# Filling TensorE's longest planned pauses with products that nobody reads, in a kernel whose order is written by a planner

## The chip, the core and the metric

The kernel runs on one core of one Trainium2 chip. The metric is the device time of one execution in microseconds (us). The median of six runs before the change is 1732.15 us, and the six lie between 1729.69 and 1736.9 us. One further execution was recorded by the hardware profiler, and every row below is from it.

The names of the engines are those of the profile: PE is TensorE's matmul unit and PEld its weight load, DVE is VectorE, ACT is ScalarE, POOL is GpSimd, SP is SyncE, which issues most DMAs. POOL issues the indirect DMAs (gathers by a list of row numbers).

## The reference

Four layers run over 64 sequences of 64 tokens, 128 features wide (4096 tokens). Each layer adds a gated cross-attention over a context and then a gated feed-forward network (FFN):

```
x = x + tanh(g_xattn[l]) * attention_l(layernorm(x), context)
x = x + tanh(g_ffn[l])   * ffn_l(layernorm(x))            # l = 0, 1, 2, 3
```

Layers 0 and 1 attend with 16 heads, layer 2 with 8, layer 3 has a resampler that attends to context and latents together. The FFNs are mixtures of experts: layer 0 has 32 small experts with 6 of them per token, layer 1 and layer 2 have 8 with 2 per token, layer 3 has 4 with 2 per token and a layernorm inside each. All of it is float32.

## The kernel before

The 4096 tokens are cut in 8 blocks of 512 (4 tiles of 128 tokens). `attention_16`, `gated_ffn`, `attention_8`, `attention_lat` and `ffn_3` each do one layer's step for one block. `sparse_ffn`, the FFN of layer 1, works on a group of two blocks, four groups in all. It sorts the tokens by expert with small matrix products and DVE operations (`slots_of`): the last of these products, `pid`, sums 16 products of 128x128 with 128x24 and gives the list `z_rows`, by which POOL gathers the rows of each expert into `zs`. TensorE transposes `zs` (into `pt`), multiplies it with the expert's weights (`g`, `u`, `po`), the result goes to DRAM (`oD`), and later 16 gathers per group fetch the results `back`.

**The planner.** No engine is called at once. The `Plan` object records every operation, and at the end `order()` simulates the five engines with costs written in the kernel: it takes the next operation of each engine by a key, holds tiles back until a buffer is free, charges 1.5 times for TensorE in the first 3.4 us after a pause of over 1.7 us, and notes when each operation would start (`starts`). An operation is one call or one `unit` of several calls on one engine, for example the four transposes of a block; its `us` is the sum of the calls' planned costs. `issue()` then calls the engines in the order of the planned starts:

```
    def issue(self):
        with self.tc.manual_schedule():
            for i in self.order():
                for bound, args, kw in self.ops[i].calls:
                    bound(*args, **kw)
```

Each engine works through its own instructions strictly in that order. An instruction waits on semaphores for its inputs and for the release of the buffer that it writes. Since all calls to the engines are made in this one place, almost every row of the profile has line L435, and rows are told apart by the names of the tiles.

**PSUM.** TensorE writes to PSUM. `ps(name)` takes one of six banks of 128x512 float32, `ps_two` the one double bank of the attention scores. A bank goes back to the pool when its last reader is done. The names that matter below: `pc` is the transposed context of a block, `pt` holds transposes, `pvar` the variances of the last FFN, `ph` its hidden layer, `po` an output projection, `g` and `u` the two halves of a gated hidden layer, and `acc` the running output of an FFN.

**How a product looks in the profile.** A float32 product takes two rows of PE and two of PEld (two passes); a transpose takes one. `masks` is a constant tile whose first 128 columns are the identity.

Of the kernel before, what the change touches and what calls it, by code (L numbers as in the profile page):

```python
# [20 lines left out]
P = 128  # L21
# [162 lines left out]
class Plan:  # L184
# [244 lines left out]
        return "no operation can start:\n" + "\n".join(lines)  # L429

    def issue(self):
        with self.tc.manual_schedule():
            for i in self.order():
                for bound, args, kw in self.ops[i].calls:
                    bound(*args, **kw)  # L435


SWITCH = 3.0
COLD, PAUSE, SLOWER = 3.4, 1.7, 1.5


class PlanEngine:
# [14 lines left out]
def flamingo_kernel(ctx: ExitStack, tc: tile.TileContext, a: dict, out: bass.AP):  # L457
    nc = Plan(tc)
# [37 lines left out]
    def load(name, shape=None, at=0.0, t=None):  # L496
        src = a[name]
        if t is None:
            t = const.tile(list(shape or src.shape), F32, tag=name, name=name, bufs=1)
        nc.sync.dma_start(t[: src.shape[0]], src, not_before=at)  # L500
        return t
# [14 lines left out]
    def source_tile(name):  # L516
        t = const.tile([C + 1, TOK], F32, tag=name, name=name)
        nc.gpsimd.memset(t[C : C + 1, :], 1.0)
        return t
# [14 lines left out]
    with nc.stage(0.0, 1.0):  # L534
# [4 lines left out]
        masks = load("masks")  # L539
# [46 lines left out]
        load_ffn(3, at=T_LOAD + 150)  # L586

    with nc.stage(0.0, 1.0):
        ident = masks[:, 0:128]
        head8 = masks[:, 128:136]  # L590
        half2 = masks[:, 136:138]
        ones = const.tile([P, P], F32, tag="ones", name="ones")
        nc.vector.memset(ones, 1.0)
        zeros = const.tile([1, 1], mybir.dt.bfloat16, tag="zero", name="zero")
        nc.vector.memset(zeros, 0.0)
        zero = zeros.to_broadcast([1, 512])
        minus_half = const.tile([P, 16], F32, tag="minus_half", name="minus_half")
        nc.vector.memset(minus_half, -0.5)

        cn_tiles = [source_tile(f"cn{i}") for i in range(2)]  # L600
        ctx_tiles = [source_tile(f"ctx{i}") for i in range(2)]
        cn_d = dram.tile([C, B * S], F32, tag="cn_d", name="cn_d", bufs=1)
        y_d = dram.tile([P, B * S], F32, tag="y_d", name="y_d", bufs=1)
        k8_d = dram.tile([P, 4 * B * S], F32, tag="k8_d", name="k8_d", bufs=1)
        v8_d = dram.tile([P, 4 * B * S], F32, tag="v8_d", name="v8_d", bufs=1)
        gates = const.tile([P, 8], F32, tag="gates", name="gates")
        nc.scalar.activation(gates, rows[:, 0:8], AF.Tanh)
# [1280 lines left out]
```

## Time and profile before

| what | value |
|---|---|
| median of the runs | 1732.15 us |
| the profiled execution, its own time | 1730.78 us |
| its span, first to last instruction | 1729.0 us |
| PE busy | 1587.9 us, 92% of the span, 14369 rows |
| DVE, POOL, ACT busy | 61%, 54%, 50% |
| mean granted TensorE clock | 0.961 |

The profiled execution's own time is 1.78 us over its span and 1.37 us under the median, so that a difference worked out on its rows can be added to the median. PE's share of busy time is an average over stages. In the page's 40 slices of 43 us PE is at 0.9 or more nearly everywhere, and falls to 0.6 to 0.8 in the first slice, in five slices from about 735 to 950 us, and in the last two. "Granted clock" is the share of full speed that the throttle gave TensorE; in the trace it takes two values, 1 and one half.

### The profile page before, as it was taken

The page shows a single profiled execution, that of the slowest core. Times are in us where ns is not written, and L with a number is a line of the kernel's source. Part 1 is how long each engine was busy: PE and PEld are TensorE (multiplying, and loading weights), DVE is VectorE, ACT ScalarE, POOL GpSimd, SP SyncE. Part 2 cuts the span into 40 slices and gives each one's busy share as a digit, 9 for nine tenths or more (in the row PEclk, how much of TensorE's full clock was granted, in tenths as well). Part 3 has the DMA queues.
Part 4 walks back from the last instruction along what each step waited for, and adds up shares of the span by engine and source line. Part 5 has one row for each costly group of instructions (what it writes and reads, how often), then busy time and mean ns, then how long its engine had stood idle before and what let it go on. Part 6 is the DMA issues. An engine that isn't in the chain of part 4 may idle for free. (4 is left out here: it accounts for less than half of the span.)

```text
span 1729.0 us, 37328 instructions
## 1 busy us (share of the span) xinstructions
PE 1587.9 (92%) x14369; PEld 1096.0 (63%) x14369; DVE 1063.3 (61%) x2933; ACT 858.5 (50%) x1289; POOL 928.8 (54%) x906
## 2 busy tenths in 40 slices
PE   6999999999999999978769599999999999899976
PEld 3556556556566656557758487766767786677654
DVE  5864777786678565762746366684655475575652
ACT  3563776666757575622324264444443553454422
POOL 7464555565654745322373555686553666654741
PEclk9999999999999999988889799999999999999998
DMA  7231160324030321465577362521152323220211
GB/s 230 96 118 60 59 192 27 117 98 119 27 123 30 102 85 55 154 205 126 148 231 192 100 215 53 181 95 56 37 159 88 103 63 117 83 89 2 81 32 38
DMA packets 107786, 180.94 MB, mean 105 GB/s; under 512 B 22964, under 2 KB 53016, under 8 KB 103128
## 3 DMA queue, kind: packets, MB, share of 16 engines
q1 hardware_dynamic: 102488, 168.06, 30.7%
q0 software_dynamic: 5120, 10.50, 3.1%
q8 instruction: 113, 1.85, 0.5%
q14 instruction: 65, 0.53, 0.1%
HBM read 146.71 MB, written 35.26 MB: 105 GB/s over the span
## 5 line engine op out<-in xcount | busy, mean ns | idle before, releaser
L435 DVE TENSOR_TENSOR h<-h,u 128x512 f32<-128x512 f32 x224 | 150.9, 685 | 216.8 <-PE u L435 137.4
L435 POOL TENSOR_TENSOR h<-h,pb 128x512 f32<-128x512 f32 x128 | 161.3, 1273 | 199.5 <-DVE h L435 99.6
L435 ACT ACTIVATE h<-g 128x512 f32<-128x512 f32 x224 | 132.6, 597 | 229.3 <-PE g L435 202.0
L435 ACT ACT_TABLE_LOAD x159 | 204.0, 1283 | 29.6 <-issue 9.1
L435 POOL TENSOR_TENSOR ln_r<-ln_ve,minus_half 128x4 f32<-128x4 f32 x64 | 66.7, 1042 | 215.6 <-DVE ln_ve L435 214.2
L435 PEld LDWEIGHTS acc<-w_L,h 128*128 128x128 f32 x1088 | 134.9, 191 | 42.6 <-issue 29.8
L435 PEld LDWEIGHTS acc<-L_w,h 128*128 128x128 f32 x1088 | 133.6, 192 | 33.0 <-issue 24.2
L435 PE MATMUL acc<-w_L,h 128*128 128x128 f32 x1088 | 144.2, 278 | 0.9 <-POOL h L435 0.7
L435 PE MATMUL acc<-L_w,h 128*128 128x128 f32 x1088 | 142.5, 278 | 0.8 <-issue 0.4
L435 PE MATMUL g<-zTm,w_L 128*128 128x512 f32 x272 | 141.8, 604 | 0.3 <-ACT cn L435 0.3
L435 PE MATMUL u<-zTm,w_L 128*128 128x512 f32 x272 | 140.1, 599 | 0.1
L435 DVE TENSOR_REDUCE top<-sc 128x16 f32<-128x1024 f32 x80 | 97.5, 1218 | 63.7 <-PE sc L435 32.7
L435 POOL TENSOR_TENSOR kb<-kT,masks 128x1024 f32<-128x1024 f32 x64 | 120.9, 1904 | 24.3 <-ACT kT L435 8.6
L435 POOL DMA_INDIRECT zs<-zD,z_rows x96 | 92.7, 965 | 75.3 <-DVE z_rows L435 23.8
L435 POOL TENSOR_SCALAR z<-x,ln_mv,ln_r 128x128 f32<-128x128 f32 x160 | 127.9, 811 | 4.4 <-DMA zs<-cT 0.8
L435 ACT COPY prT<-pt 128x512 f32<-128x512 f32 x176 | 95.9, 593 | 46.8 <-PE pt L435 44.1
L435 POOL TENSOR_TENSOR pb<-zTm,pb 128x512 f32<-128x512 f32 x64 | 80.0, 1271 | 45.3 <-DMA pb<-cD 43.3
L435 ACT ACTIVATE pr<-pr 128x1024 f32<-128x1024 f32 x88 | 93.0, 1057 | 17.0 <-DVE pr L435 16.2
L435 PEld LDWEIGHTS pt<-masks,pr 128*128 128x128 f32 x704 | 80.1, 142 | 31.7 <-issue 21.5
L435 PE MATMUL pt<-masks,pr 128*128 128x128 f32 x704 | 97.3, 276 | 2.8 <-POOL pr L435 1.0
L435 POOL TENSOR_TENSOR pr<-pr,rs 128x512 f32<-128x512 f32 (+1 forms) x40 | 47.8, 1211 | 81.3 <-DVE rs L435 59.2
L435 POOL DMA_INDIRECT back<-oD,rows_of x64 | 63.2, 988 | 44.0 <-issue 25.0
(299 smaller groups left out, 3381.0 us busy)
## 6 DMA issues: line engine op xcount, KB each, us to landing
wt<-experts SPq DMA_DIRECT2D x96, 384.0 KB
pb<-cD SPq DMA_DIRECT2D x256, 128.0 KB
pb<-cD SPq DMA_DIRECT2D x96, 256.0 KB
k_d<-kS SPq DMA_DIRECT2D x8, 1024.0 KB
v_d<-vS SPq DMA_DIRECT2D x8, 1024.0 KB
kT<-k_d SPq DMA_DIRECT2D x8, 1024.0 KB
v<-v_d SPq DMA_DIRECT2D x8, 1024.0 KB
oD<-zs SPq DMA_DIRECT2D x32, 192.0 KB
```

Of the source, the lines that this page charges most:

```text
L435: bound(*args, **kw)
```

## The change

`issue()` keeps the planned end of the last TensorE operation (`done`). Before each TensorE operation it looks at the planned pause since then. If the pause is 3.0 us or longer, the tile that the operation writes first has two dimensions, and the operation doesn't add to an earlier sum, then `keep_busy` issues int((pause - 1.0) / 0.25) products ahead of it. Each multiplies the identity with itself (128 rows by up to 128 columns on both sides) and is written to the first columns of the bank that the operation writes next, which overwrites it. No other operation, order or cost is changed, and the planner doesn't know of the products.

```
     def issue(self):
+        done = 0.0
         with self.tc.manual_schedule():
             for i in self.order():
-                for bound, args, kw in self.ops[i].calls:
+                op = self.ops[i]
+                if op.eng == "PE":
+                    if done > 0.0:
+                        self.keep_busy(op, self.starts[i] - done)
+                    done = self.starts[i] + op.us
+                for bound, args, kw in op.calls:
                     bound(*args, **kw)
+
+    def keep_busy(self, op, pause):
+
+        dst = op.calls[0][1][0]
+        if pause < LONG or len(dst.shape) != 2 or not op.calls[0][2].get("start", True):
+            return
+        m, n = dst.shape[0], min(dst.shape[1], P)
+        for _ in range(int((pause - IDLE) / FILL)):
+            self.tc.nc.tensor.matmul(
+                dst[:, 0:n], lhsT=self.filler[:, 0:m], rhs=self.filler[:, 0:n], start=True, stop=True
+            )
 
 
 SWITCH = 3.0
 COLD, PAUSE, SLOWER = 3.4, 1.7, 1.5
+LONG, IDLE, FILL = 3.0, 1.0, 0.25
...
-        ident = masks[:, 0:128]
+        ident = nc.filler = masks[:, 0:128]
```

## The prediction

> **What bounds the kernel now.** The page first, then TensorE's waits, then its timeline around the longest of them.
>
> ```profile
> PE 1587.9 (92%) x14369; PEld 1096.0 (63%) x14369; DVE 1063.3 (61%) x2933; ACT 858.5 (50%) x1289; POOL 928.8 (54%) x906
> PEclk9999999999999999988889799999999999999998
> ```
>
> TensorE is the bound nearly everywhere. Its idle time is 1729.0 - 1587.9 = 141 us. A clock of 0.961 means (1 - 0.961) x 2 x 1729 = 135 us at half speed, so better warmth could never give more than 67 us. The waits (us in total, times, longest):
>
> ```profile
> PE g L435 <- ACT zs L435: 17.0, 5, 14.9
> PE ph L435 <- DVE zs L435: 15.4, 2, 8.1
> PE pt L435 <- DMA zs<-zD,z_rows: 10.6, 3, 6.5
> PE pid L435 <- issue: 8.5, 1, 8.5
> ```
>
> Which pauses are filled follows from the planner's starts, which the kernel before computes too. Eight planned pauses last 3 us or more; one (`pv` in `context_8`) has three dimensions and drops out. The other seven, in order, with planned pause and number of products, and in brackets TensorE's real pause there: A `pc` of block 0, 5.1 us, 16 (0.4 at 9.54 us); B `pid` of the second group, 9.7 us, 34 (8.49); C the next `pt`<-`zs`, 10.4 us, 37 (6.53); D a `pt` of `attention_8`, 4.1 us, 12 (none, at 989.96); E a `pvar`, 4.5 us, 14 (0.1, at 1598.83); F a `ph`, 7.5 us, 25 (8.10, at 1673.64); G the last such `ph`, 6.6 us, 22 (7.26, at 1704.13). That is 160 products, 320 rows. In all but A, whose bank is new, and E, the bank's last reader ends before TensorE falls idle, so the products start at once.
>
> When does the clock fall? The granted clock changes on a grid of 3.41 us; these stretches are such windows (columns: length, busy time by engine, clock):
>
> ```profile
> 905.50:908.90 3.40, 1.38 (x6) 0.55 (x5) 0.91 (x6) 3.36 (x5) 1.89 (x2) 1.00 0.65 162
> 1417.50:1420.90 3.40, 1.99 (x7) 0.79 (x5) 3.12 (x17) 0.58 (x2) 0.10 (x2) 1.00 0.69 77
> 1670.10:1673.50 3.40, 0.00 (x0) 0.00 (x0) 0.68 (x1) 0.00 (x0) 3.32 (x5) 0.50 0.76 242
> 1673.50:1677.00 3.50, 3.36 (x4) 1.40 (x5) 2.09 (x4) 0.60 (x1) 3.48 (x4) 0.51 0.18 67
> ```
>
> After the first (PE busy 1.38 of 3.40, 41%) the next window is at half, after the second (59%) it isn't. After one window that is full (the last) the clock is back. So TensorE must be busy for about half of every window.
>
> Around B and C (first DVE, which needs `pid`; then PE alone):
>
> ```profile
> 868.21 0.18 DVE L435 CAST z_rows<-pid 128x24 int32<-128x24 f32 x1 [7.18 <-remote]
> ```
>
> ```profile
> 846.94 1.16 PE L435 MATMUL acc<-shared,h 128*128 128x128 f32 x8
> 856.59 6.99 PE L435 MATMUL pid<-ids,match 128*128 128x24 f32 x32 [8.49 <-issue]
> 863.41 2.05 PE L435 MATMUL acc<-shared,h 128*128 128x128 f32 x8
> 872.00 0.48 PE L435 MATMUL pt<-masks,zs 128*128 128x128 f32 x1 [6.53 <-DMA zs<-zD,z_rows]
> 874.11 0.48 PE L435 MATMUL pt<-masks,zs 128*128 128x128 f32 x1 [1.64 <-issue]
> 877.65 0.47 PE L435 MATMUL pt<-masks,zs 128*128 128x128 f32 x1 [3.07 <-DMA zs<-zD,z_rows]
> ```
>
> `pid` ends at 863.58, yet DVE sees it only at 868.21. POOL runs 16 `back` gathers without a break from 845.41 to 866.02. The same beside another run of gathers (801.90 to 809.19), where TensorE had nothing to wait for:
>
> ```profile
> 804.95 0.65 PE L435 MATMUL av<-prT,values 128*32 128x64 f32 x32
> 805.42 0.40 PE L435 MATMUL av<-prT,sums_w 128*32 128x128 f32 x6
> 806.13 0.39 PE L435 MATMUL av<-prT,sums_w 128*32 128x128 f32 x2 [0.32 <-issue]
> 807.55 0.38 PE L435 MATMUL av<-prT,sums_w 128*32 128x128 f32 x2 [1.03 <-issue]
> 808.97 0.38 PE L435 MATMUL av<-prT,sums_w 128*32 128x128 f32 x2 [1.04 <-issue]
> 810.37 0.67 PE L435 MATMUL av<-prT,sums_w 128*32 128x128 f32 x4 [1.02 <-issue]
> ```
>
> In the middle of one unit TensorE drops to two rows per 1.42 us, and recovers 1.2 us after the last gather. I counted its rows from the first gather of a run until this starts: 53 here, 57 from 1110.09, 50 from 1432.59, 48 from 946.95, 49 from 941.08, 72 from 1178.36. So beside a run of gathers TensorE gets about 50 rows, then crawls, and its results are seen late. What holds it, the trace doesn't say.
>
> **The change part by part.** A pass of 128x128 starts every 0.1115 us at full clock and 0.213 at half (`acc` rows); one product costs 0.223 or 0.427 us. Nothing is removed or moved.
>
> A. The clock is at half there until 24.9 us. 16 products cost 6.8 us cold, about 5.8 if the clock rises on the way, so `pc` ends near 15.6 instead of 10.8. ACT's copy of it (12.35) already waited for the DMA of `rows`, so that copy slips 3.5 us. The next TensorE work, `pk`, `pv`, `pz` (5.2 us cold, 2.5 warm), ran until 18.0 and then waited for the DMA of weights until 20.23. This wait is the cover: warm, TensorE is through by 18.8. If the clock is still up at 20.23, the `pk` products behind it save up to 2.3 us; if all stays cold, they start 2 us late. Range -2.3 to +2.0; taken 0, between ends with nothing to choose.
>
> B. 12 rows fall between the first gather (845.41) and 848.1, so about 40 of the 68 new rows run densely, until 852.6; then two per 1.42 us until 867.2 gives 20. Left then: 8 new rows and the 32 of `pid` behind them, cold, 40 x 0.216 = 8.6, ending at 875.8 instead of being seen at 868.2: +7.6. With a crawl of three rows per 1.25 us (that from 1436) 35 rows pass, 25 are left: 5.4 us, +4.4. Without the crawl `pid` isn't late at all: 34 x 0.223 = 7.6 us end at 855.7, before `match` is ready; `pid` would be faster, but DVE's wait to 868.2 hides it: 0. Range 0 to +7.6; taken +6, between the two crawls. Queued behind: the shared `acc`, DVE's `z_rows`, POOL's nine gathers of `zs`.
>
> C. These gathers (11.0 us long) then start near 874.7, and TensorE, free near 876, runs 74 rows beside them. About 45 pass before the crawl: 16 cold rows (3.4 us) and 29 warm (3.2) reach 882.6; crawling until 1.2 us after the gathers, 886.9, gives 6; the other 23 need 2.6 to 4.9, so `pt` is free at 889.5 to 891.8. The third `pt` was due at 877.65 + 6 = 883.65: +5.9 to +8.2. Without the crawl 16 cold and 58 warm rows end at 885.8, +2.1; with B at nothing, they end before 872, 0. Behind it lie TensorE pauses of 1.64 (894.4) and 2.11 (906.9) that can take up to 3.7. Range 0 to +8; taken +3, the crawl less that cover.
>
> D. No pause here, and the planner was wrong by all of it: 12 x 0.223 = 2.7 us ahead of transposes that TensorE was ready for, 5.1 if wholly cold. From there to 1112 TensorE idles about 1.3 us, so nearly all passes on. Range +1.4 to +5.1; taken +2.5.
>
> E. 14 x 0.223 = 3.1 us, from 1598.83 to 1601.95. Cover: the first `pvar` ran alone and the other three waited until 1601.05 for DVE's `q`; unhindered, all four take 1.06 us (1657.64), so they end at 1603.0, before 1603.3. Taken 0; without that cover +3.1.
>
> F and G. 5.6 and 4.9 us of products in pauses of 8.10 and 7.26 leave 2.5 and 2.4 us idle. Each window needs about half its length busy, and such a tail takes over half of one window in most positions of the grid. Warm, F would gain 1.2 (then POOL's `z` limits it, 1675.8) and G 1.8. Range -3.0 to 0 together; taken -1.0.
>
> The Trainium skill, in "TensorE: Matmul & The Clock Gate", section "Why this matters for your kernels", advises against TensorE gaps of more than about 3 us between bursts, since an idle window halves the clock. By it F and G would win their full 3.0 us; the 41% row says that a part-filled window falls too, so the -1.0 stands on that. "Runtime: NRT & Kernel Launch", section "Instruction fetch mechanics", says that an engine streams its instructions ahead and that refills are mostly hidden. By it extra rows never run TensorE dry, and B and C would be 0; the `av` rows above show TensorE running dry of something, so I go by them.
>
> Sum: 0 + 6 + 3 + 2.5 + 0 - 1.0 = +10.5; I take off 1 for later pauses that absorb some, +9.5. On the profiled execution: 1730.78 + 9.5 = 1740.3; on the median: 1732.15 + 9.5 = 1741.6.
>
> **Rivals.** *No crawl* (0.18): the products are not held, B and C cost nothing, D less F and G remain: +1.5, 1733.7. For it: `pid` and `acc`, 40 rows, ran beside the `back` gathers unhindered. Against: 12 + 40 is 52, just the limit.
>
> *The clock decides* (0.08), faster: `pid` warm takes 3.5 us instead of 7.0. If `z_rows` really waits for `pid`'s own end, that end comes at 860.1 instead of 868.2: -8; with A -2.3 and F and G -3.0, against D +2.5: -10.8, 1721.3. It decides as soon as `z_rows` follows `pid` by its usual 0.2 us. Against: the first group's `z_rows` did so, but the second's, beside gathers, came 4.6 us late.
>
> *The pauses aren't there* (0.06): all 160 products lie on the path, 160 x 0.223 = +35.7, 1767.9. Against: four of seven pauses are real.
>
> **How the numbers follow.** Forecast 0.68 (+4 to +19: B and C at their ends, D at 1.4 to 5). 0.2% of 1732 is 3.5 us, about what can be told from no change. Slower by more: 0.68 + 0.06 + 0.03 of *no crawl*; within: 0.13; faster: 0.08 + 0.02, *no crawl* with A, F and G at their best. The range leaves out *the clock decides*, *the pauses aren't there* and the far end of the forecast: 1731 to 1751.
>
> **What would show it.** Right: 320 more PE rows; `pid`'s 32 rows torn apart near 853 to 875 with gaps at POOL's rhythm; `z_rows` 4 to 8 us later after the last `back` gather; `pt`<-`zs` delayed by `pt`<-`masks`; 24 new rows directly ahead of the `pt` at D; `pvar`'s end unmoved; `ph` at F and G still at half clock. Wrong: the 68 rows at B packed in 7.6 us with `pid` behind them on time, or a clock well above 0.965.

## The result

The changed kernel takes 1738.9 us (median of 25 runs, 1733.05 to 1746.71). The kernel before, run beside it and before it, takes 1732.24 us (51 runs, 1720.9 to 1738.63). The ratio is 1.0040, with a 95% interval of 1.0028 to 1.0052: slower by 6.9 us, 4.9 to 9.0. The profiled execution took 1734.12 us, with a span of 1732.3 us and a clock of 0.969; it is one of the shortest runs of its kernel, and the profile of before lay near its median, so the two spans differ by only 3.3 us.

The profile after, first the page:

```profile
PE 1611.7 (93%) x14689; PEld 1128.7 (65%) x14689; DVE 1067.4 (62%) x2933; ACT 859.0 (50%) x1289; POOL 931.2 (54%) x906
PEclk9999999999999999978889799999999999999999
```

There are exactly 320 more PE rows, and PE is busy 23.8 us longer. The idle time fell from 141 to 120.6 us, the clock rose from 0.961 to 0.969, and the kernel still became slower. TensorE's waits (us in total, times, longest) say where. The new rows have line L450.

```profile
PE g L441 <- ACT zs L441: 24.0, 6, 16.2
PE pid L450 <- issue: 11.6, 9, 1.9
...
PE ph L441 <- DVE zs L441: 5.1, 2, 2.7
```

The 15.4 us ahead of `ph` (F and G) shrank to 5.1, since products fill them. In the place of the 8.5 us ahead of `pid` stand nine waits of the *filler rows themselves*, 11.6 us, that nothing in the profile explains ("issue"). PE's timeline at B and C:

```profile
847.09 6.71 PE L450 MATMUL pid<-masks 128*128 128x24 f32 x50
854.48 0.20 PE L450 MATMUL pid<-masks 128*128 128x24 f32 x1 [0.68 <-issue]
855.92 0.20 PE L450 MATMUL pid<-masks 128*128 128x24 f32 x1 [1.24 <-issue]
857.32 0.20 PE L450 MATMUL pid<-masks 128*128 128x24 f32 x1 [1.21 <-issue]
...
866.44 0.20 PE L450 MATMUL pid<-masks 128*128 128x24 f32 x1 [1.19 <-issue]
867.16 2.31 PE L450 MATMUL pid<-masks 128*128 128x24 f32 x10 [0.53 <-issue]
869.30 7.00 PE L441 MATMUL pid<-ids,match 128*128 128x24 f32 x32
876.13 2.06 PE L441 MATMUL acc<-shared,h 128*128 128x128 f32 x8
877.98 8.47 PE L450 MATMUL pt<-masks 128*128 128x128 f32 x71
886.80 0.49 PE L450 MATMUL pt<-masks 128*128 128x128 f32 x3 [0.35 <-issue]
```

Fifty filler rows run densely. Then one row passes per 1.2 to 2.1 us until about 2.5 us after the last `back` gather (they run from 844.57 to 864.60). The real `pid` waits in the same queue, starts 12.7 us later than before and ends at 876.3. DVE's next step:

```profile
876.34 0.18 DVE L441 CAST z_rows<-pid 128x24 int32<-128x24 f32 x1 [13.00 <-PE pid L441]
```

Against the last `back` gather this is 11.7 us behind, where it was 2.2 us before. At C, 71 rows ran densely beside the `zs` gathers and only a few stood. At the other places:

```profile
15.89 0.60 PE L441 MATMUL pc<-masks,c_in 128*96 128x128 f32 x4
...
20.29 3.70 PE L441 MATMUL pk<-c,L_k 96*128 96x512 f32 x8 [0.34 <-DMA L_k<-in_L_k]
```

The last of these rows was, before:

```profile
20.23 6.00 PE L435 MATMUL pk<-c,L_k 96*128 96x512 f32 x8 [2.23 <-DMA L_k<-in_L_k]
```

At A `pc` starts 6.35 us later, the wait for the weights' DMA shrinks from 2.23 to 0.34 us, and the `pk` products behind it take 3.70 us warm for 6.00 cold (warm and cold: at full and at half clock).

```profile
993.72 3.38 PE L450 MATMUL pt<-masks 128*128 128x128 f32 x24
996.93 1.04 PE L441 MATMUL pt<-masks,pr 128*128 128x128 f32 x8
```

At D the 24 rows lie directly ahead of the transposes. F and G, after and then before:

```profile
1678.67 1.98 PE L441 MATMUL ph<-zs,L_w 128*128 128x512 f32 x4 [2.73 <-DVE zs L441]
...
1707.60 3.22 PE L441 MATMUL ph<-zs,L_w 128*128 128x512 f32 x4 [2.40 <-DVE zs L441]
```

```profile
1673.64 3.60 PE L435 MATMUL ph<-zs,L_w 128*128 128x512 f32 x4 [8.10 <-DVE zs L435]
1704.13 3.71 PE L435 MATMUL ph<-zs,L_w 128*128 128x512 f32 x4 [7.26 <-DVE zs L435]
```

F's `ph` ran warm, G's mostly cold, with nearly the same idle tail of 2.4 to 2.7 us.

I set the end of each TensorE operation against the same one before. The differences in this one profile: -2.2 us behind A (26 us), -5.9 by 783, -0.8 at 848, the last row ahead of the pause, **+12.7 at `pid`** (a jump of 13.6), +10.4 at `pt`, +3.8 at 990, +6.5 behind D, +4.3 at 1483, +4.8 ahead of F, +3.4 behind it, +3.3 at the end.

### The profile page after: what moved, and what is told of

It reads as the page before. It is cut to its first block, busy times and chain, and to the rows that moved or that the text cites. A ratio compares the mean times of both kernels' runs of the same rounds, so it can differ in the third digit from the quotient of the medians.

```text
span 1732.3 us, 37969 instructions
## 1 busy us (share of the span) xinstructions
PE 1611.7 (93%) x14689; PEld 1128.7 (65%) x14689; DVE 1067.4 (62%) x2933; ACT 859.0 (50%) x1289; POOL 931.2 (54%) x906
```

## The experiments

All kernels use this edit, with a table of products by place (1 is A, 7 is G), and two of them add a few lines. The table of all seven is the change itself.

```
+FILLS = {1: 16, 2: 34, 3: 37, 4: 12, 5: 14, 6: 25, 7: 22}
...
-        for _ in range(int((pause - IDLE) / FILL)):
+        self.place = getattr(self, "place", 0) + 1
+        for _ in range(FILLS.get(self.place, 0)):
```

The experiments fell on three chips, and this matters: on one the kernel before takes 1671.6 us (I call it the quick chip), on the two others 1735.0 or 1733.3, and 1730.74 us. Each ratio is against runs of before on the same chip. The quick chip was used for one group of runs only, so what is put down to the chip below could also be its state at that time; the runs don't tell these apart.

### Each part alone, on the quick chip

**B alone**, `FILLS = {2: 34}`.

> Only the 34 products at B are left. Theory 1 (products beside POOL's gathers crawl): the filler rows run densely for about 8 us after the first `back` gather, then one or two per gather until some 2 us after the last one, so that `pid` ends about 12 to 14 us later and `z_rows` is written 7 to 9 us later than before; TensorE's later pauses up to 990 us give back half, and +3 to +5 us is left at the end. Theory 2 (B is hidden: `z_rows` and the gathers behind it have room, and the loss of the whole change is D's and scatter): `pid` is late but the end moves by less than 1.5 us.

Measured 1.0001 (0.9985 to 1.0016). The rows:

```profile
832.60 12.50 PE L451 MATMUL pid<-masks 128*128 128x24 f32 x68
844.93 7.00 PE L441 MATMUL pid<-ids,match 128*128 128x24 f32 x32
```

No gap at all, although 16 `back` gathers run from 830.08 to 850.68, 1.25 us each as before: 68 filler rows and `pid` run straight through. DVE writes `z_rows` at 851.97, right at `pid`'s end. Theory 1's crawl does not exist on this chip. Nor is the filler free: 12.5 us for 68 rows is almost all cold. Counted from the first gather, `z_rows` comes 3.7 us later than in the run of C alone, which has nothing at B (21.9 against 18.2), but the end doesn't show it: POOL is busy with the `back` gathers for 20.6 us in either run, so the `zs` gathers behind them start only 1.4 us later (22.3 against 20.9).

**C alone**, `FILLS = {3: 37}`.

> Only the 37 products at C are left. Theory 1: without B they start at about 865.5 us, 3 us ahead of the first of the nine `zs` gathers, so that only about 59 rows fall beside gathers; in the changed kernel 76 rows passed beside nine gathers before TensorE stood still, so they are through by about 877 us, when the third `pt` was due before, and the products behind run warm: -2 to +1 us at the end. Theory 3 (the limit is about 50 rows, as I had counted): TensorE stands still near 876 us until 1.2 us after the last gather (881), `pt` ends 3 to 4 us later, +1 to +4 us at the end.

Measured 1.0005 (0.9991 to 1.0020). All 74 rows ran densely and the first `g` and `u` behind them were warm (0.94 and 0.83 us). That decides nothing about a limit, since no row is held on this chip. The run shows one more thing: `z_rows` starts at 845.49, with the end of `pid` and 2.4 us ahead of the end of the last `back` gather (847.89). So nothing in the program makes `z_rows` wait for these gathers; on the slower chip it comes 2.2 us behind them all the same.

**D alone**, `FILLS = {4: 12}`.

> Only the 12 products at D are left. Theory 1: 24 rows warm, 2.7 us, ahead of transposes that are ready, with almost no TensorE pause behind them: +2 to +3 us at the end. Theory 4 (pauses beside the gathers near 1117 and 1190 us take it up): less than +1 us.

Measured 1.0015 (1.0001 to 1.0029), that is +2.5 us (0.2 to 4.8), the size of 24 rows, though the lower end lies within theory 4. And in this profile the transposes behind D waited 3.4 us for POOL's `pr` afterwards, so that the rows were covered where they lie. The time fits theory 1 best; the trace of this chip doesn't show why.

**A, F and G alone**, `FILLS = {1: 16, 6: 25, 7: 22}`.

> Only the products at A (16), F (25) and G (22) are left. Theory 1: A lifts the clock before the `pk` products of the weights and gains 2.2 us as in the changed kernel's profile, F about 1, G nothing, so -2 to -4 us at the end. Theory 5 (A's gain is taken up by the waits for gathers near 780 us, where the changed kernel's profile falls from 5.9 us ahead to 1.4 us ahead): only F is left, -0.5 to -1.5 us.

Measured 0.9975 (0.9958 to 0.9993), -4.2 us (1.2 to 7.0): a gain clear of noise, the size of theory 1, with the far end of theory 5 just inside the interval. The products away from gathers gain. What A and what F and G give of it, the time doesn't tell; the profiles do, below.

### The whole, and B alone, on a slower chip

**The whole**, all seven counts.

> The changed kernel once more (same instructions, the counts written in a table). The runs of B, C, D and A+F+G alone fell on a chip where the kernel before takes 1671.6 us and TensorE didn't stand still beside gathers in any of the four traces. Theory 6 (the crawl belongs to a chip, and with it the loss): on a chip with the kernel before near 1672 us the ratio is that of the parts, about 0.9999 (B 1.0001, C 1.0005, D 1.0015, A+F+G 0.9975 together: 0.9996), and no gaps stand in the rows of `pid`; on one near 1732 us it is 1.003 to 1.005 with gaps. Theory 7 (the loss is that of the whole, the parts hide it): 1.003 or more on either.

Measured 1.0052 (1.0031 to 1.0073) against 1735.0 us. 61 rows passed from the first gather to the first gap, then one at a time; `z_rows` came 10.6 us behind the last gather. Theory 6 said 1.003 to 1.005 with gaps on such a chip, and that is what came. The other half of it, about 0.9999 for the whole on the quick chip, was not run. A has the `pk` products at 3.70 us again. F and G, with the same counts, were both cold this time.

**B alone** once more, `FILLS = {2: 34}`.

> Only B once more. On a chip where the kernel before is near 1732 us, theory 1: gaps of 1 to 2 us between the filler rows from some 8 us after the first `back` gather, `z_rows` 7 to 9 us later, ratio 1.002 to 1.004. On one near 1672 us: no gaps, ratio 0.9985 to 1.0015 as before.

Measured 1.0055 (1.0030 to 1.0079): B alone costs +9.5 us (5.2 to 13.7), all that the whole change costs and above the 1.004 that I expected at most.

```profile
851.06 6.27 PE L451 MATMUL pid<-masks 128*128 128x24 f32 x49
857.86 0.20 PE L451 MATMUL pid<-masks 128*128 128x24 f32 x1 [0.53 <-issue]
859.28 0.20 PE L451 MATMUL pid<-masks 128*128 128x24 f32 x1 [1.23 <-issue]
...
871.38 1.92 PE L451 MATMUL pid<-masks 128*128 128x24 f32 x9 [1.90 <-issue]
873.12 7.00 PE L441 MATMUL pid<-ids,match 128*128 128x24 f32 x32
```

```profile
880.16 0.18 DVE L441 CAST z_rows<-pid 128x24 int32<-128x24 f32 x1 [16.00 <-PE pid L441]
```

Again 61 rows to the first gap, and `z_rows` 11.0 us behind the last gather's end (869.17). The same kernel gave 1.0001 on the quick chip. So the loss is B's, and it comes with the crawl. A fetch of instructions by DMA doesn't explain the gaps: from 864 to 871 us, while rows still stood for up to 1.9 us, no packet of an instruction queue moved, and the rows ran on at 871.38 without one.

### Why rows are held: fewer rows, longer rows, no gathers

On the same slower chip.

**12 products at B**, `FILLS = {2: 12}`.

> Only B, with 12 products (24 rows) for 34. Theory 8 (the limit is a number of rows, about 60 from the first `back` gather: 60 in the runs of all seven and of B alone on the slower chip): 12 rows lie between the first gather and the pause, 24 are new, so 24 of the 32 rows of `pid` still run densely and 8 crawl at about 1.4 per gather until some 866 us in the time of before; `z_rows` moves by -1 to +2 us, the ratio is 0.999 to 1.001. Rival (any filler there costs the same, as the clock or the bank does it): `z_rows` 5 us later or more, ratio 1.003 or more. On a chip with the kernel before near 1672 us: nothing either way.

```profile
849.83 2.76 PE L451 MATMUL pid<-masks 128*128 128x24 f32 x24
858.40 7.03 PE L441 MATMUL pid<-ids,match 128*128 128x24 f32 x32 [5.81 <-DVE match L441]
865.25 0.56 PE L441 MATMUL acc<-shared,h 128*128 128x128 f32 x1
867.30 0.37 PE L441 MATMUL acc<-shared,h 128*128 128x128 f32 x1 [1.49 <-issue]
868.73 0.37 PE L441 MATMUL acc<-shared,h 128*128 128x128 f32 x1 [1.06 <-issue]
```

Now it isn't the filler that is held, nor `pid`, but the `acc` behind it: the first gap comes after 69 rows. `z_rows` comes 2.5 us behind the last gather, as before (2.2). So the place is as theory 8 said. The time isn't: 1.0025 (1.0009 to 1.0041), where I expected at most 1.001. Set against before, `acc` ends 6.1 us later and `pid` just ahead of it 1.8, so the hold costs `acc` 4.3 us, and `pt`, waiting for its DMA, covers most of it. By 985 us the difference is 0.5. It grows to +10 only behind 1112 us, where nothing was added, and it grows there in the profile of the next kernel too (+11 at the end), whose time is that of before. So the profile shows no loss at B, and where the 4 us of the ratio come from stays open.

**9 long products at B**, 128x512 into the whole bank.

```
+        nc.wide = getattr(nc, "wide", []) + [pid[:, 0:512]]
...
+            wide = next(t for t in self.wide if t.tensor is dst.tensor)
             self.tc.nc.tensor.matmul(
-                dst[:, 0:n], lhsT=self.filler[:, 0:m], rhs=self.filler[:, 0:n], start=True, stop=True
+                wide, lhsT=self.filler[:, 0:m], rhs=self.filler[:, 0:1].to_broadcast([P, 512]), start=True, stop=True
```

> Only B, with 9 products of 128x512 into the whole bank of `pid` for 34 of 128x24: the same 7.7 us of TensorE, 18 rows for 68. Theory 8 (rows count, not time): 12 + 18 + 32 = 62 rows, so that at most the last few of `pid` crawl; `z_rows` -1 to +2 us, ratio 0.999 to 1.001. Rival (TensorE's busy time beside the gathers counts): gaps between the wide rows or in `pid` from the middle of the gathers on, `z_rows` 5 us later or more, ratio 1.003 to 1.006 as with 34 small ones.

```profile
851.95 7.92 PE L452 MATMUL pid<-masks 128*128 128x512 f32 x18
860.52 4.79 PE L441 MATMUL pid<-ids,match 128*128 128x24 f32 x32 [0.65 <-issue]
865.14 1.81 PE L441 MATMUL acc<-shared,h 128*128 128x128 f32 x6
868.00 0.37 PE L441 MATMUL acc<-shared,h 128*128 128x128 f32 x1 [1.06 <-issue]
```

These products take 7.9 us of TensorE, about the 7.7 that the 34 short ones were reckoned at, in 18 rows for 68, and nothing is held until 68 rows have passed. The ratio is 0.9998 (0.9985 to 1.0011), the time as expected. Here `pid` starts half warm and takes 4.79 us for 7.0, but this brings nothing: DVE writes `z_rows` at 872.48, 2.4 us behind the last gather, as with 12 products (2.5).

**34 products, plain copies for the 16 gathers.** The rows copied are rows 0 to 127, not those listed.

```
+                    if op.calls[0][0].__name__ == "indirect_dma_start" and args[2].shape[0] == SLOT_TILES * P:
+                        self.backs = getattr(self, "backs", 0) + 1
+                        if self.backs <= 16:
+                            bound = lambda dst, _, src, rows: self.tc.nc.gpsimd.dma_start(dst, src[0:P, :])
                     bound(*args, **kw)
```

> B with its 34 products, and the 16 `back` gathers beside them made plain copies of the first 128 rows, issued by POOL too (the rows fetched are not the listed ones: that part of the computation is left out). Theory 9 (POOL's gathers hold TensorE): no gap in the 68 rows, `pid` follows within 8 us of the first and `z_rows` within 0.3 us of `pid`'s end. Rival (what holds TensorE is something else at this place, its own supply of instructions or the transfers of the expert weights): the gaps stay, after some 60 rows.

```profile
839.17 7.70 POOL L444 DMA_DIRECT2D back<-oD  x14
847.28 1.08 POOL L444 DMA_DIRECT2D back<-oD  x2 [0.41 <-DMA back<-oD]
```

```profile
854.24 10.24 PE L455 MATMUL pid<-masks 128*128 128x24 f32 x68
864.31 7.00 PE L445 MATMUL pid<-ids,match 128*128 128x24 f32 x32
871.13 2.05 PE L445 MATMUL acc<-shared,h 128*128 128x128 f32 x8
```

No gap, on the chip that shows them otherwise, and `z_rows` is written at 871.35, at `pid`'s own end: theory 9. Without POOL's gathers neither the rows nor the signals are held. But the copies didn't take the gathers' place in time: POOL took 9.2 us for all 16, where the gathers take 20.6, and was through at 848.36, 5.9 us ahead of the first filler row. So the 68 rows ran beside nothing of POOL's. What ran beside the copies were 73 other rows of TensorE from 839.17 on, with one break over 0.2 us among them, a wait for ACT's `zs`. (`pid` follows 10 us after the first row, not 8, since the rows turned cold.) The expert weights move at the same time at about 300 GB/s, so it isn't these transfers. This is one run without an interval, and its time isn't used.

The same profile shows something about the clock. Its columns are length, busy time of PE, PEld, DVE, ACT and POOL, granted clock, DMA share and GB/s; the rows lie on the grid of the clock:

```profile
859.00:862.40 3.40, 3.40 (x19) 3.40 (x18) 3.30 (x8) 0.00 (x0) 0.00 (x0) 0.50 0.89 298
862.40:865.80 3.40, 3.40 (x17) 3.40 (x18) 3.37 (x10) 0.00 (x0) 0.00 (x0) 0.50 0.97 303
865.80:869.20 3.40, 3.40 (x17) 3.40 (x18) 1.31 (x8) 0.00 (x0) 0.00 (x0) 0.50 0.97 353
```

TensorE is busy 3.40 us of 3.40 in three windows running, the clock fell ahead of the first (at 859.0) with TensorE busy, and it stays at half. All of these rows have 24 columns.

### The better version

**A, F and G, these two filled to the end**, `FILLS = {1: 16, 6: 36, 7: 32}`, on a slower chip beside the whole and B.

> Only A (16), F and G, and these two filled to the end of the real pause (36 and 32 products, 8.0 and 7.1 us by 0.223 us each, where the change has 25 and 22). Theory 1: no window at half clock is left at F and G, `ph` takes 1.7 to 2.0 us at both, 1.5 to 3 us better than A+F+G with the counts of the change: ratio 0.996 to 0.9975. Rival: `ph` waits for DVE's `zs`, and what the products take over its time delays it, so no better than 0.9975.

```profile
1678.93 1.98 PE L441 MATMUL ph<-zs,L_w 128*128 128x512 f32 x4
...
1708.01 1.98 PE L441 MATMUL ph<-zs,L_w 128*128 128x512 f32 x4 [0.30 <-DVE zs L441]
```

Both `ph` are warm. The ratio is 0.9970 (0.9953 to 0.9988), -5.2 us, within the range of theory 1; the rival, a delayed `ph`, isn't seen. Against before, TensorE gains 3.3 us from the last row ahead of F to the end, where the counts of the change gave 1.5 and nothing in two profiles. That the full filling is better by the time isn't shown: 0.9975 with the smaller counts was measured on the quick chip, and the intervals overlap.

**The same once more**, beside the next kernel.

> A, F and G alone once more, F and G filled to the end (16, 36 and 32 products), beside the next kernel on the same chip: ratio 0.996 to 0.998 on either kind of chip. If the first result was a draw of the chip, 0.999 or more.

Measured 0.9955 (0.9940 to 0.9970) on a third chip, 1724.7 against 1730.74 us, a little better than the range expected. F and G give 3.3 us again. It isn't a draw of the chip. This kernel beats the kernel before on both chips, and the change where they ran side by side.

**A, F, G and 30 products at C**, `FILLS = {1: 16, 3: 30, 6: 36, 7: 32}`.

> The same with 30 products at C. Without B, some 45 of these 60 rows fall beside the nine `zs` gathers, under the limit of about 60, so nothing is held; they raise the clock ahead of the first `g` and `u`, which took 1.65 and 1.49 us in the profile before and take 0.94 and 0.83 warm: 1 to 2.5 us better than without C, ratio 0.995 to 0.9975. Rival (C costs what I had predicted of it, 3 us): 0.998 to 1.000, with `pt` held until after the last gather.

```profile
867.45 7.69 PE L451 MATMUL pt<-masks 128*128 128x128 f32 x52 [0.84 <-issue]
874.99 0.38 PE L441 MATMUL pt<-masks,zs 128*128 128x128 f32 x2
877.37 0.33 PE L441 MATMUL pt<-masks,zs 128*128 128x128 f32 x1 [2.00 <-issue]
881.65 0.58 PE L441 MATMUL g<-zs,wt 128*128 128x128 f32 x1 [3.95 <-ACT zs L441]
```

A miss. The first 8 rows bring the count from the first `back` gather to 60, and there TensorE stands for 0.84 us, until 2.0 us behind the last of these gathers. The 52 behind them pass densely, and the last `pt` ends at 877.7 as it did without C. But ACT copies it only at 881.12, 2.0 us behind the last `zs` gather (879.07), and `g` then starts 3.6 us later than in the kernel without C, cold again. So there is a price at the place, the 3 us of the rival. Over the whole kernel 0.9968 (0.9954 to 0.9982) can't be told from 0.9955.

## Why the prediction was right, and where it wasn't

**The whole.** Predicted 1741.6 (1731 to 1751), slower by 9.5 us. Measured 1738.9, slower by 6.9 (4.9 to 9.0), and by 9.0 (5.4 to 12.7) on the chip with the whole and B. The likeliest case was the one that came, for the reason given: B's rows are caught beside the gathers and hold `pid`. Of the signs named ahead, the 320 rows, the delayed `pt`, the rows at D and the unmoved `pvar` came. Not so: `pid`'s own 32 rows were not torn apart but ran densely behind the torn filler, `z_rows` came more than 8 us later, and F's `ph` was warm in one of two profiles.

**B was mis-sized, +6 for about +9.** The steps: 40 rows dense, then 20 crawling, 40 left, `pid` at 875.8. The trace: 50 dense, then 8 in about 13 us, 42 left, `pid` at 876.3, with gathers that began 0.8 us earlier. The crawl is one row per gather, where I took the two or three that the `av` rows show, and the dense part is longer, 61 or 62 rows from the first gather for 50. The two errors cancel in `pid`'s end; but measured from the gathers, DVE's step is 8.4 to 9.6 us later in three profiles, above my limit of +7.6. That limit held the end of the gathers to be 1.2 us ahead of recovery, as at 809 to 810; it was 1.8 to 2.6 us. So that the number for the whole came out near is in part luck.

**The price of a warm row, 0.1115 us, was wrong at B.** The clock falls while these 24-column rows run, in all five profiles with 34 products there. The trace of before had shown it: `pid` and `acc` ran from 856.59 to 865.46, through two whole windows, and the clock stayed at half until 881.7. I had read only the `ph` window, 512 columns wide, and concluded that one full window brings the clock back and that half a window of any rows keeps it up. The Trainium skill, in "TensorE: Matmul & The Clock Gate", section "What's actually happening", says that the monitor sets the clock by how busy TensorE has recently been, and that one busy window releases it. "Busy" in the profile's sense isn't that: the three rows above are 100% busy at 0.50.

**C was mis-sized the other way, +3 for 0 to 1 at the end of its stage.** Counted from `z_rows`, the last of the three `pt` ends 12.2 and 12.5 us later in the two profiles of the whole, 7.3 us later with B alone and 9.9 us later before. So C delays it by 5 us against B alone and by 2.3 to 2.6 against before, not by 5.9 to 8.2: I had put the crawl after 45 rows, and about 76 passed. The `g` and `u` behind it are warm (0.94 and 0.83 us, against 1.65 and 1.49 with B alone), which I hadn't counted in this case; against B alone 2.9 us are left at the end of the next `pt`, and by 911 us none or one. Without B it costs 3.6 us at the place, through a signal that is seen late and not through held rows.

**A: 0, measured -2.2 and -3.1** in two profiles (`pk`'s end), the gainful end of my bounds. All of the chain through ACT slipped into the wait for the weights' DMA, as the terms said; of the two ends I had no reason to choose, and the rise of the clock before 20.23 us decided.

**D: +2.5, measured +2.8 and +2.7** in the two profiles. **E: 0**; the difference is the same ahead of it and behind it (+4.3 and +4.3, +10.3 and +10.3). **F and G: -1.0, measured -1.5 and about 0**, against before; three profiles without products there lie 0.3 to 1.9 us above before from F to the end, so that this size is known only to within some 2 us. F was warm or cold by where the grid of the clock falls on the idle tail, as the step said, and G cold in both. Filling to the end takes the tail away.

**What later pauses absorb, 1 us,** was not a constant: from `pid` to the end the difference fell by 9.4 us in the first profile, by 1.9 in the second of the whole (D, F and G lie in between in both) and by 2.2 with B alone.

**The rivals.** *No crawl* is how B behaves on the quick chip, where its ratio is 1.0001. I had put it down to the limit of rows; but 100 rows ran there beside 16 gathers without a stall, so it goes with the chip. *The clock decides* fell on the slower chip because `pid` rows that are partly warm (4.79 us) don't make `z_rows` earlier: it is seen 2.4 us behind the last gather whether `pid` is early or not. I had given that as the reason against it, from one place of the trace. On the quick chip, where `z_rows` does follow `pid`, the filler left `pid` cold (7.00 us), so there the rival is untested.

**Open.** What the gathers take from TensorE, and why one chip is free of it. The same skill page, in "Architectural detail: the array is 16× 32×32, not 1× 128×128", gives TensorE's queue 64 entries, and 60 to 69 rows passed before the first gap at B. That suggests a queue that runs empty and isn't refilled beside gathers. It is a guess: nothing here tests it, each of these rows comes with a row of weight load, so that the instructions are twice as many, at C about 76 passed, and beside the other run of 16 `back` gathers, at about 940 to 980 us, 36 to 56 passed in eight profiles ahead of the first stall. Not explained either: the 4 us of B with 12 products, and D's cost where the trace covers it.

## What to carry to other kernels

A filler instruction is not free because the engine is idle: it sits in the queue ahead of the work that the pause was waiting for, and whatever slows the queue there (here POOL's gathers, after some 60 rows) is paid by that work. Fill pauses whose *measured* length is known, away from such neighbours, and to the end: F and G gave 3.3 us so. A place without a pause can pay too, where a later wait covers the products and what follows runs at a better clock: A gave 2.2 to 3.1 us. Together they gave 5 to 8 us, and B alone lost more than that. Beside gathers few long products are better than many short ones: 9 for 34 cost nothing at B. And look at the same kernel on several chips before a difference of half a per cent is put down to the code.

## What the runs showed of the hardware

- The same program took 1671.6 us on one chip and 1731 to 1735 on others, 3.5% more. In the quick chip's profiles no row is held beside the gathers up to 990 us (100 rows pass beside the 16 at B), and the stretch from 750 to 990 us of before, where the gathers are, is about 50 us shorter.
- On the slower chips TensorE gets 60 to 69 rows from the first of the 16 `back` gathers at B on, whether these have 24, 128 or 512 columns, then about one per gather, and its signals are seen 2.0 to 2.5 us behind the last gather. Beside other runs of gathers the first stall comes after 36 to 76 rows. Without the gathers nothing is held, and beside 16 plain copies issued by POOL 73 rows passed.
- Products of 24 columns don't keep the clock up: three windows at 100% busy, granted clock 0.50. Products of 128x512 at the same place kept it up until 863.0, 2.5 us after the 24-column rows of `pid` began, and 128x128 ones raised it at A.
